# Neighbourhood attention in blocks of 8x8 queries of two heads, inside a kernel of attention and state-space layers

## The chip, the cores and the metric

The kernel runs on one core of one Trainium2 chip. The core has five engines that run side by side, each with its own queue in fixed order: TensorE (PE, matrix products; its weight loads are shown apart as PEld), VectorE (DVE), ScalarE (ACT), GpSimd (POOL) and SyncE (SP, which here only issues transfers). The metric is the device time of one launch in microseconds (us), as the median of several runs.

## The reference

```python
x = x + L0(_gn(x), w_qkv, w_out)      # x: (2, 48, 48, 768) float32
x = x + L1(_gn(x), in_proj_w, ...)    # group norm over 32 groups of 24 channels
...
# L0: 12 heads of 64; each query sees a 7x7 window of keys, clipped at the image's edge
scores = jnp.einsum('nhije,nhiajbe->nhijab', q, kg)
attn = jax.nn.softmax(scores.reshape(B, nh, H, W, K * K), axis=-1)
o = jnp.einsum('nhijab,nhiajbe->nhije', attn, vg)
return o @ w_out
...
# L1, for both directions of the 2304 tokens, 1536 channels, 16 states:
#   x, z = in_proj(x); x = silu(causal conv of 4 taps)
#   delta = softplus(dt_proj(x_proj(x)))
h = dA * h + (d_t * u_t)[..., None] * B_t[:, None, :]
y = jnp.einsum('bdn,bn->bd', h, C_t)
#   out = out_proj((y_forward + y_backward) * silu(z))
```

## The kernel before

**Order.** The kernel does not issue its work as it goes. Every piece of work is handed to a planner (class `Order`, line 94) with its engine, a cost in ns, a key (its due place, counted in units of the scan), and the buffers that it reads and writes. `Order.run` (line 153) then simulates the engines on these costs, and of the works that are ready takes the one that can start first, with the lower key ahead; works marked `job` fill in beside the main ones, but none more than 2.5 units ahead of the main work (`horizon`, line 170). The result is one fixed order of instructions on each engine. Where the planner sees PE without work for over 0.8 us in the scan, it puts idle transposes there (line 1491). On the chip, semaphores alone decide when an instruction starts; a fetch into a fresh buffer waits for nothing but its place in SP's queue.

**Stages.** Image 0's group norm and attention come first, with nothing beside them. Then DVE and POOL run the scan of image 0, forward and backward (1152 scan instructions of two states each on DVE, line 1258), and beside much of it, as jobs, the whole attention of image 1 (keys 50 to 118 units, `A1`) and then image 1's input projection and convolution (`in_proj`, from unit 118). Then the scan of image 1 follows, 1152 more. A scan unit is one channel tile of 128 in one chunk of 384 tokens: four groups of four states. In each group DVE or POOL fills `hb` (line 1225; the planner may choose the engine), ACT makes the decays in PSUM (line 1247), DVE scans, POOL multiplies by C (line 1273), and PE adds up by transposes into `py` (line 1290).

**Attention** (line 529). For every band of eight image rows (`t`, six bands, 384 queries) `project` makes queries, keys and values by matmuls (`product`, line 382) and spills them to HBM. `core(t)` goes over three groups `g` of two head pairs; it loads 14 rows of keys for the group (line 671) and its queries, and calls `block` for three blocks `u` of 8x16 queries. A block sees 14x22 = 308 keys, in three chunks of five, five and four rows (110, 110 and 88 keys). `block` fetches the values of the chunks (line 740) and a mask of 128 x 308 (line 751), and calls `heads` for each of the two head pairs. `heads` works on the two heads of a pair apart, each with 128 queries on the partitions:

- scores (line 769): one matmul for each head, 64 rows of the array, 128 queries by 308 keys, each head into a PSUM bank of its own
- DVE adds the mask and takes the minimum of the negated sum (line 779), ACT takes exponentials with their sum (line 785), DVE inverts the sum (line 800), DVE (image 0, line 816) or ACT (image 1, line 810) scales
- PE transposes three chunks a head into a bank (line 825); ACT copies the first two, and DVE (image 0) or ACT (image 1) the third (line 832)
- values (line 856): three chunks by two heads, each matmul 64 channels by 128 queries; the copy of the result is line 866

So each pair and block is two masks, two exponentials, two scalings, four copies, six transposes. For image 0 scores have both banks of `das[0]`, and transposes both of `das[1]` (`two`, line 536); for image 1 all share the tag `mm` with two banks, and scores and transposes take two of them at a time. Values of image 1 lie in the `uz` buffers beside the keys.

After the core, line 382 with `mm_ao` is the output projection, line 705 adds the input, line 710 takes statistics for the next group norm.

**Group norm** (line 427). Statistics of all tiles are aggregated (line 443); PE sums the channels of a group by a first matrix `gs` (line 448), and spreads the group's mean and later its scale back over channels by a second one, `gT` (line 457), which SP fetches (line 431). The planner lets that fetch follow the aggregation.

Of the kernel before, what the change touches and what calls it, by code (L numbers as in the profile page):

```python
# [26 lines left out]
QR, QC = 8, 16  # L27
WR, WC = QR + KN - 1, QC + KN - 1
NKEY = WR * WC
KR = 5  # L30
KCH = tuple((r * WC, min(KR, WR - r) * WC) for r in range(0, WR, KR))
# [26 lines left out]
def neighbourhood_masks():  # L58


    out = np.full((3, 3, QR, QC, WR, WC), NEG, np.float32)
    for a, t in enumerate((0, 1, HW // QR - 1)):
        for u in range(HW // QC):
            kr, kc = window(t, QR, WR), window(u, QC, WC)
            for r in range(QR):
                sr = min(max(t * QR + r - KN // 2, 0), HW - KN) - kr
                for c in range(QC):
                    sc = min(max(u * QC + c - KN // 2, 0), HW - KN) - kc
                    out[a, u, r, c, sr : sr + KN, sc : sc + KN] = 0.0
    return out.reshape(9, P, NKEY)  # L70
# [175 lines left out]
def tile_kernel(  # L246
# [61 lines left out]
    def cols(l0, cl, k0=0, nk=1):  # L308
# [6 lines left out]
        "w": 5, "u": 2, "dtw": 2, "dlt": 2, "hb": 7, "uz": 2, "vt": 3, "ev": 4, "pr": 4, "pT": 2,  # L315
# [111 lines left out]
    def group_norm(stats, n, key, job):  # L427
# [62 lines left out]
        for i, (eng, ns, fn, r, w) in enumerate((  # L490
            ("DVE", 600, aggregate, [stats], [mv]),
            ("SP", 400, fetch, [mv], [gT]),
# [36 lines left out]
    def attention(b, start, end, job, T):  # L529
# [6 lines left out]
        def two(what, n):  # L536

            if T[what] == "mm":
                return [ps("mm", f"{what}{n}_{j}") for j in range(2)]
            return [(das[T[what]], j) for j in range(2)]  # L540
# [14 lines left out]
        def project(t):  # L555
# [18 lines left out]
            for p in range(NP):  # L574
                for s in range(2):
# [10 lines left out]
                    if s == 0:  # L586
# [4 lines left out]
                                e.ap.rearrange("p (u r c) -> p u r c", u=HW // QC, r=QR),  # L591
                                acc[:, :TB].rearrange("p (r u c) -> p u r c", u=HW // QC, r=QR),
# [47 lines left out]
        def core(t):  # L640
# [12 lines left out]
            for g in range(NP // PG):  # L653
# [5 lines left out]
                nv = len(KCH) * PG * P if kv else 0  # L659
                ks = sb(tag("k", g), [P, nk + nv], f"k{n}", parts=2)  # L660

                vs = [(ks, 1, nk)]
                if kv:
                    more = sb(tag("k", g), [P, (HW // QC - 1) * nv], f"kv{n}", parts=HW // QC - 1)
                    vs += [(more, u, u * nv) for u in range(HW // QC - 1)]
# [10 lines left out]
                def queries(qs=qs, rows=rows):  # L676
# [4 lines left out]
                    w=[(ks, 0), *(v[0] for v in vs[1:])], size=PG * P * WR * HW * 4, **S,  # L681
# [5 lines left out]
                for u in range(HW // QC):  # L687
                    block(t, g, u, kr, rc, near, ks, vs, qs, oT, kg + u * slot * 0.8 / NP * PG / 3)
# [32 lines left out]
        def block(t, g, u, kr, rc, near, ks, kvs, qs, oT, key):  # L721

            kc = window(u, QC, WC)
            n = f"{b}_{t}_{g}_{u}"
            if "v" in T:
                vs, v0 = (sb(tag("v", u), [P, len(KCH) * PG * P], f"v{n}"), 0), 0
            else:
                vs, v0 = kvs[u][:2], kvs[u][2]
            vat = lambda p0, p1, k, c0, c1: vs[0][
                p0:p1, v0 + k * PG * P + c0 : v0 + k * PG * P + c1  # L730
            ]
            mask = sb("mask", [P, NKEY], n)
# [3 lines left out]
            def values():  # L736
                grid = vd[b].ap.rearrange("(h w) e -> h w e", w=HW)
                for k, (c0, nk) in enumerate(KCH):
                    r0 = kr + KR * k
                    nc.sync.dma_start(  # L740
                        vat(0, nk, k, 0, PG * P),
                        grid[r0 : r0 + nk // WC, kc : kc + WC, cs],
                    )

            add(
                "SP", 400 * len(KCH), values, key - 0.5,
                r=[(vd[b], [h * NTB + x for h in halves for x in near])], w=[vs],
                size=NKEY * PG * P * 4, **S,
            )
            add(  # L750
                "SP", 400, lambda: nc.sync.dma_start(mask.ap, masks[rc * 3 + u]), key - 0.5, w=[mask],
                size=P * NKEY * 4, **S,
            )
            for i in range(PG):
                p = g * PG + i
                heads(f"{n}_{i}", p, i, u, kc, ks, qs, vs, vat, mask, oT[p], key + 0.001 * i)

        def heads(n, p, i, u, kc, ks, qs, vs, vat, mask, to, key):

            sc, pts = two("s", n), two("pt", n)  # L760
            pr = [sb("pr", [P, NKEY], f"{n}_{j}") for j in range(2)]
            pT = sb("pT", [P, len(KCH), 2, P], n, parts=2)
            sm = sb("sm", [P, 4], n, parts=4)
            grid = lambda h: ks[h, i * WR * HW : (i + 1) * WR * HW].rearrange("p (r w) -> p r w", w=HW)[:, :, kc : kc + WC]

            def scores():
                for j in range(2):
                    h = slice(j * E, (j + 1) * E)
                    nc.tensor.matmul(
                        bank(sc[j], NKEY), qs[h, i, u * P : (u + 1) * P], grid(h), start=True,  # L770
                        stop=True,
                    )

            add("PE", mm(1, NKEY) * 1.2, scores, key, r=[(ks, 0), qs], w=[*sc, *pr], **S)
            for j in range(2):

                def masked(j=j):

                    nc.vector.tensor_tensor_reduce(  # L779
                        pr[j].ap, bank(sc[j], NKEY), mask.ap, -1.0, 3.0e38, ALU.add, ALU.min,  # L780
                        sm[:, j : j + 1],
                    )

                def exponentials(j=j):
                    nc.scalar.activation(  # L785
                        pr[j].ap, pr[j].ap, AF.Exp, bias=sm[:, j : j + 1], scale=-1.0,
                        accum_out=sm[:, 2 + j : 3 + j],
                    )

                add("DVE", dve(NKEY), masked, key, r=[sc[j], mask], w=[pr[j], (sm, j)], **S)  # L790
                add(
                    "ACT", act(NKEY, 1) + 90, exponentials, key, r=[pr[j], (sm, j)],
                    w=[pr[j], (sm, 2 + j)], **S,
                )

                if j or not job:
                    of = range(2 if job else 2 + j, 3 + j)
# [7 lines left out]
            for j in range(2):  # L805
                if job:

                    add(
                        "ACT", act(NKEY, 1),
                        lambda j=j: nc.scalar.mul(pr[j].ap, pr[j].ap, sm[:, 2 + j : 3 + j]), key,  # L810
                        r=[pr[j], (sm, 2 + j)], w=[pr[j]], **S,
                    )
                else:
                    add(
                        "DVE", 300,
                        lambda j=j: nc.vector.tensor_scalar_mul(
                            pr[j].ap, pr[j].ap, sm[:, 2 + j : 3 + j]
                        ),
                        key, r=[pr[j], (sm, 2 + j)], w=[pr[j]], **S,
                    )  # L820
                pt = pts[j]

                def turned(j=j, pt=pt):
                    for k, (c0, nk) in enumerate(KCH):
                        nc.tensor.transpose(  # L825
                            bank(pt, 512 - P)[:nk, k * P : (k + 1) * P], pr[j][:, c0 : c0 + nk],
                            ident,
                        )

                def taken(ks, copy, j=j, pt=pt):  # L830
                    nk = KCH[ks.start][1]
                    copy(
                        pT[:nk, ks, j, :],
                        bank(pt, 512 - P)[:nk, ks.start * P : ks.stop * P].rearrange(
                            "p (k q) -> p k q", q=P
                        ),
                    )

# [703 lines left out]
```

## Time and profile before

| | us |
|---|---|
| median of 3 runs (lowest, highest) | 7038.78 (7036.31, 7051.21) |
| the profiled execution: its span, from first to last instruction | 7054.5 |
| DVE, PE, POOL, ACT busy in the span | 6061.2, 6334.5, 5447.5, 4970.2 |
| scan, line 1258: 2304 x 1.746 us | 3924.9 |
| POOL's multiplication, line 1273: 1152 x 3.186 us | 3653.7 |
| fills, line 1225: POOL 495 x 3.203 us, DVE 657 x 1.743 us | 1584.6, 1141.4 |
| idle transposes, line 1491: 4431 | 550.4 |

The profiled execution is 15.7 us longer than the median of the runs. Its own time is known by its span only. In the profile a group is a line, an engine and an operation, with the names of output and inputs; a bracket behind an instruction gives the idle time of its engine before it and what ended that time. PE's ends are modelled, so that neighbours overlap a little: cadences are taken from start to start. A window row gives, for each engine, the busy time in the stretch and the number of instructions.

### The profile page before, as it was taken

The numbers are of one execution on the slowest core, as the hardware profiler recorded it, in microseconds if no ns is written. First come the engines' busy times: TensorE is split into PE (matmuls) and PEld (weight loads), VectorE is DVE, ScalarE is ACT, GpSimd is POOL, SyncE is SP. The second block draws the span as 40 slices with busy tenths as digits, with TensorE's granted clock in tenths as the row PEclk, the third lists the DMA queues.
The fourth block names the chain that finished last, engine by engine and source line by source line (L and its number), as shares of the span: only waits on it lengthen the run. The fifth ranks groups of instructions, "written<-read, shape, count | busy, mean of one in ns | idle before, by whom it ended". The sixth has DMA issues, their size and how long they took to land.

```text
span 7054.5 us, 105645 instructions
## 1 busy us (share of the span) xinstructions
PE 6334.5 (90%) x38151; PEld 4844.6 (69%) x38151; DVE 6061.2 (86%) x6217; ACT 4970.2 (70%) x10948; POOL 5447.5 (77%) x1951
## 2 busy tenths in 40 slices
PE   7999989999989998999988888888888898999888
PEld 5666656666667776676666656666678887777777
DVE  2354449999999999998898999999999999999998
ACT  1333248788887788887888778788876667777765
POOL 0000008888989999988898878999999999999997
PEclk9999989999999999999999999999999999999999
DMA  6565454444556444555444354343466676655553
GB/s 190 172 200 172 139 161 131 134 144 151 157 160 191 151 149 141 152 170 150 126 144 131 113 166 127 107 143 108 140 179 191 174 220 199 191 177 158 162 169 105
DMA packets 1337698, 1101.32 MB, mean 156 GB/s; under 512 B 136328, under 2 KB 1327416, under 8 KB 1337144
## 3 DMA queue, kind: packets, MB, share of 16 engines
q1 hardware_dynamic: 1337176, 1094.56, 52.1%
q8 instruction: 303, 4.96, 0.3%
q14 instruction: 219, 1.79, 0.1%
HBM read 881.41 MB, written 213.57 MB: 155 GB/s over the span
## 4 chain that ended last, share of the span: by engine, by line
DVE 39%; PE 19%; ACT 14%; POOL 12%; issue 9%; DMA 6%; SPq 1%; DVEq 0%; POOLq 0%; ACTq 0%
DVE hb L1258 25%; POOL hb L1273 8%; DVE hb L1225 7%; ACT da L1247 4%; PE mm_qk L382 4%; DVE uz_u L935 4%; POOL hb L1225 3%; PE py L1290 2%; PE mm_ao L382 2%; PE mm_v L382 2%; PE mm_xin L382 2%; ACT uz_u L928 1%; PE da L825 1%; ACT pr L785 1%; ACT L1163 1%
## 5 line engine op out<-in xcount | busy, mean ns | idle before, releaser
L1258 DVE TENSOR_TENSOR_SCAN hb<-da,hb 128x772 f32<-128x772 f32 x2304 | 3924.9, 1746 | 187.3 <-ACT da L1247 155.1
L1273 POOL TENSOR_TENSOR hb<-hb,bc 128x1536 f32<-128x1536 f32 x1152 | 3653.7, 3186 | 381.0 <-DVE hb L1258 338.3
L1247 ACT ACTIVATE da<-dlt,A 128x384 f32<-128x384 f32 x4608 | 2677.2, 584 | 915.2 <-DVE hb L1258 845.8
L1290 PE MATMUL py<-ident,hb 128*128 128x128 f32 x13824 | 1754.3, 279 | 264.3 <-POOL hb L1273 255.2
L1290 PEld LDWEIGHTS py<-ident,hb 128*128 128x128 f32 x13824 | 1570.9, 143 | 523.5 <-POOL hb L1273 413.6
L1225 POOL TENSOR_TENSOR hb<-u,bc 128x1544 f32<-128x1544 f32 x495 | 1584.6, 3203 | 22.6 <-PE py L1290 14.9
L1225 DVE TENSOR_TENSOR hb<-du,bc 128x1544 f32<-128x1544 f32 x657 | 1141.4, 1743 | 34.3 <-ACT du L1202 24.8
L1175 POOL TENSOR_TENSOR u<-dlt,u 128x384 f32<-128x384 f32 x288 | 263.8, 918 | 532.7 <-DMA bc<-xdf 412.6
L382 PE MATMUL mm_xin<-xc,w_x 128*128 128x390 f32 x1656 | 593.3, 504 | 25.3 <-DVE uz_u L935 16.2
L382 PE MATMUL mm_z<-xc,w_z 128*128 128x384 f32 x1728 | 608.1, 492 | 7.8 <-ACT dlt L1157 4.9
L382 PE MATMUL mm_out<-stage_y,w_o 128*128 128x192 f32 x3168 | 560.7, 332 | 18.1 <-ACT dlt L1157 6.4
L1491 PE MATMUL py<-ident 128*128 128x128 f32 x4431 | 550.4, 277 | 0.0
L382 PEld LDWEIGHTS mm_out<-stage_y,w_o 128*128 128x128 f32 x3168 | 522.0, 194 | 29.3 <-ACT dlt L1157 10.6
L1491 PEld LDWEIGHTS py<-ident 128*128 128x128 f32 x4431 | 503.3, 143 | 28.9 <-issue 26.0
L901 POOL MEMSET xc<- 128x18 f32 x4 | 0.5, 116 | 637.2 <-DVE sm L779 637.2
L382 PEld LDWEIGHTS mm_xin<-xc,w_x 128*128 128x128 f32 x1656 | 311.3, 195 | 238.3 <-issue 36.7
L935 DVE SCALAR_TENSOR_TENSOR uz_u<-mm_xin,conv_w,uz_u 128x384 f32<-128x384 f32 x792 | 428.3, 607 | 52.0 <-ACT uz_u L928 49.4
L382 PE MATMUL mm_qk<-xc_xn,w_qk 128*128 128x384 f32 x1296 | 459.1, 500 | 14.7 <-DMA w_qk<-in_w_qkv 3.1
L382 PEld LDWEIGHTS mm_z<-xc,w_z 128*128 128x128 f32 x1728 | 314.3, 192 | 194.4 <-issue 8.9
L382 PEld LDWEIGHTS mm_qk<-xc_xn,w_qk 128*128 128x128 f32 x1296 | 240.2, 194 | 173.8 <-issue 19.5
L785 ACT ACTIVATE pr<-pr,sm 128x308 f32<-128x308 f32 x432 | 234.5, 544 | 127.5 <-DVE sm L779 127.2
L1306 PE MATMUL py<-ident,vt 128*128 128x128 f32 x864 | 156.3, 292 | 146.3 <-ACT yt L1316 145.9
(163 smaller groups left out, 6780.9 us busy)
## 6 DMA issues: line engine op xcount, KB each, us to landing
w_o<-in_w_opT SPq DMA_DIRECT2D x264, 384.0 KB
bc<-xdf SPq DMA_DIRECT2D x96, 768.0 KB
bc<-xdb SPq DMA_DIRECT2D x96, 768.0 KB
w_qk<-in_w_qkv SPq DMA_DIRECT2D x144, 384.0 KB
w_x<-in_w_inT SPq DMA_DIRECT2D x144, 384.0 KB
w_z<-in_w_inT SPq DMA_DIRECT2D x144, 384.0 KB
w_ao<-in_w_out SPq DMA_DIRECT2D x72, 384.0 KB
u<-uf SPq DMA_DIRECT2D x48, 576.0 KB
```

The lines of the kernel that those rows point to most:

```text
L382: nc.tensor.matmul(acc[:m, o0 : o0 + cl], wb[:, wi, wo : wo + m], xb[:, xi, xo : xo + cl], start=c == 0, stop=c == n - 1,)
L785: nc.scalar.activation(pr[j].ap, pr[j].ap, AF.Exp, bias=sm[:, j : j + 1], scale=-1.0, accum_out=sm[:, 2 + j : 3 + j],)
L825: nc.tensor.transpose(bank(pt, 512 - P)[:nk, k * P : (k + 1) * P], pr[j][:, c0 : c0 + nk], ident,)
L935: nc.vector.scalar_tensor_tensor(u, px[:, at[j] : at[j] + cl], q["conv_w"][:, k, j : j + 1], u, ALU.mult, ALU.add,)
L1175: lambda j=j: nc.gpsimd.tensor_mul(u[:, j, h], dl[:, j, c], u[:, j, h]), at + 0.06 + 0.25 * j,
L1225: on.tensor_mul(cells(hb, SG), by.unsqueeze(1).to_broadcast([P, SG, W]), bc[g].ap)
L1247: lambda: nc.scalar.activation(cells(da, 2)[:, j % 2, h], dl[:, jd, c], AF.Exp, scale=q["A"][:, k, i : i + 1]),
L1258: lambda: nc.vector.tensor_tensor_scan(flip(hb[at2]), flip(da[:, : 2 * W]), flip(hb[at2]), 0.0, ALU.mult, ALU.add),
L1273: lambda: nc.gpsimd.tensor_mul(cells(hb, SG)[:, :, h], cells(hb, SG)[:, :, h], bc[NSG + g][:, :, c]),
L1290: nc.tensor.matmul(py[:tp, t * P : (t + 1) * P], cells(hb, SG)[:, j, h][:, tb[t]], ident, start=False, stop=g == NSG - 1 and j == SG - 1 a ...
L1306: nc.tensor.matmul(py[:tp, t * P : (t + 1) * P], vt[:, tb[t]], ident, start=t == 0, stop=False, is_transpose=True, skip_group_check=True,)
L1491: nc.tensor.matmul(marks["py"][:, CL : CL + P], ident, ident, start=False, stop=False, is_transpose=True, skip_group_check=True,)
```

## The change

Blocks become 8x8 queries with 14x14 = 196 keys in two chunks of seven rows (98 keys). The 64 queries of both heads of a pair stand together on the 128 partitions. `heads` handles two neighbouring blocks (`UU = 2`) at a time, so that it still covers 8x16 queries of a head pair, and `block` is called as often as before.

- Scores are four matmuls of 64 queries by 196 keys. The two heads use different rows and columns of the array, and write to different halves of the partitions of one bank, in which both blocks lie.
- Masks, exponentials and scalings stay two for each call, each 128 x 196 in place of 128 x 308; two inverses are as before.
- Four transposes take the place of six. Their copies are one of 512 columns on ACT (image 1), or one of 256 on ACT and one of 256 on DVE (image 0), in place of four.
- The value matmuls are eight, 64 channels by 64 queries, in place of six, 64 by 128.
- Scores and transposes take one bank each (`one`): of `das` in turn, or one of the tag `mm`.
- Value fetches are four of 98 keys in place of three; the mask is 128 x 392. For image 1 three of the twelve value pieces lie beside the keys and nine in the second buffer.
- `pr` has three buffers, each for both blocks, in place of four for one head each. The planner's costs for these works are changed with them.
- In the group norms of image 0, the fetch of `gT` follows a given tile's statistics (`near`) and not the aggregation.

```diff
-QR, QC = 8, 16
+QR, QC = 8, 8
+NQ = QR * QC
+NU = HW // QC
...
-KR = 5
-KCH = tuple((r * WC, min(KR, WR - r) * WC) for r in range(0, WR, KR))
+KR = 7
+KCH = tuple((r * WC, KR * WC) for r in range(0, WR, KR))
+NK = len(KCH)
+UU = 2
...
-    def group_norm(stats, n, key, job):
+    def group_norm(stats, n, key, job, near=None):
...
-            ("SP", 400, fetch, [mv], [gT]),
+            ("SP", 400, fetch, [mv] if near is None else [(stats, near)], [gT]),
...
-        def two(what, n):
+        def one(what, n):
 
             if T[what] == "mm":
-                return [ps("mm", f"{what}{n}_{j}") for j in range(2)]
-            return [(das[T[what]], j) for j in range(2)]
+                return ps("mm", f"{what}{n}")
+            i = turns[what] = turns.get(what, -1) + 1
+            return das[T[what]], i % 2
...
             def scores():
-                for j in range(2):
-                    h = slice(j * E, (j + 1) * E)
-                    nc.tensor.matmul(
-                        bank(sc[j], NKEY), qs[h, i, u * P : (u + 1) * P], grid(h), start=True,
-                        stop=True,
-                    )
+                for v in range(UU):
+                    for j in range(2):
+                        h = slice(j * E, (j + 1) * E)
+                        at = (u * UU + v) * NQ
+                        nc.tensor.matmul(
+                            scv(v)[j * NQ : (j + 1) * NQ], qs[h, i, at : at + NQ], grid(h, kcs[v]),
+                            start=True, stop=True,
+                        )
...
                     nc.vector.tensor_tensor_reduce(
-                        pr[j].ap, bank(sc[j], NKEY), mask.ap, -1.0, 3.0e38, ALU.add, ALU.min,
-                        sm[:, j : j + 1],
-                    )
+                        pr[:, v, :], scv(v), mask[:, v * NKEY : (v + 1) * NKEY], -1.0, 3.0e38,
+                        ALU.add, ALU.min, sm[:, v : v + 1],
+                    )
...
+            if job:
+                add("PE", UU * NK * 110 + 60, lambda: turned(range(UU)), key, r=[pr], w=[pt, pT], **S)
+                add(
+                    "ACT", act(UU * NK * P) + 30, lambda: taken(range(UU), nc.scalar.copy), key, r=[pt],
+                    w=[pT], **S,
+                )
+            else:
+                for v in range(UU):
+                    add(
+                        "PE", NK * 120 + 60, lambda v=v: turned([v]), key,
+                        r=[(pr, v), *([pt] if v else [])], w=[pt, (pT, v)], **S,
+                    )
+                for v, (eng, copy) in enumerate((("ACT", nc.scalar.copy), ("DVE", nc.vector.tensor_copy))):
+                    add(
+                        eng, act(NK * P) + 60, lambda v=v, copy=copy: taken(range(v, v + 1), copy), key,
+                        r=[pt], w=[(pT, v)], **S,
+                    )
...
-                for k, (c0, nk) in enumerate(KCH):
-                    for j in range(2):
-                        e0 = i * P + j * E
-                        nc.tensor.matmul(
-                            po[j * E : (j + 1) * E, :P], vat(0, nk, k, e0, e0 + E), pT[:nk, k, j, :],
-                            start=k == 0, stop=k == len(KCH) - 1,
-                        )
...
+                for v in range(UU):
                     for k, (c0, nk) in enumerate(KCH):
+                        for j in range(2):
+                            e0 = i * P + j * E
+                            nc.tensor.matmul(
+                                po[j * E : (j + 1) * E, v * NQ : (v + 1) * NQ],
+                                vat(v, k, nk, e0, e0 + E), pT[:nk, v, k, j * NQ : (j + 1) * NQ],
+                                start=k == 0, stop=k == NK - 1,
+                            )
...
-        norms.append(group_norm(stats2, f"b{b}", end, job))
+        norms.append(group_norm(stats2, f"b{b}", end, job, None if b else (NC - 2) * NTB - 1))
...
-        norms0.append(group_norm(s0, f"a{b}", A0[0] - 1 + 22 * b, b > 0))
+        norms0.append(group_norm(s0, f"a{b}", A0[0] - 1 + 22 * b, b > 0, None if b else NTB - 2))
```

## The prediction

> **What bounds the kernel now.** I read the chain of work that ended last first, then busy time by stretch, then single engines. The chain over the whole span:
>
> ```profile
> DVE 39%; PE 19%; ACT 14%; POOL 12%; issue 9%; DMA 6%; SPq 1%; DVEq 0%; POOLq 0%; ACTq 0%
> ```
>
> PE's share lies mostly in the first 950 us, image 0's attention, where nothing else can run yet. There PE works without a gap in the order of its instructions (start, length, line, count):
>
> ```profile
> 521.31 0.88 PE L856 MATMUL py_po<-pT,bc_v 110*64 110x128 f32 x12
> 522.12 0.87 PE L825 MATMUL da<-ident,pr 128*110 128x128 f32 x6
> 522.91 0.79 PE L769 MATMUL da<-hb_k,bc_q 64*128 64x308 f32 x4
> 523.63 2.20 PE L382 MATMUL mm_qk<-xc_xn,w_qk 128*128 128x384 f32 x6
> ...
> 28.35 0.54 SPq L431 DMA_DIRECT2D w_gTa<-c_gmatT  x1
> ...
> 34.93 2.69 PE L457 MATMUL mm_gna<-gn_ga,w_gTa 32*128 32x1 f32 x12 [5.60 <-DMA w_gTa<-c_gmatT]
> ...
> 951.41 2.68 PE L457 MATMUL mm_gnb<-gn_gb,w_gTb 32*128 32x1 f32 x12 [5.16 <-DMA w_gTb<-c_gmatT]
> ```
>
> From start to start, one pair of heads on one block costs PE 0.81 us (values), 0.79 (transposes) and 0.72 (scores), 2.32 in all; every fp32 matmul is two records, a transpose one. Between 44.6 and 943.7 PE is busy 861.2 of 899.1 us. The last two lines are the group norms' wait for the second matrix, with no other work to cover it.
>
> After that DVE bounds, with POOL close behind (they share the fills, L1225). I cut the time of image 1's attention at scan counts (L1258), since the scans are the same before and after: 576, 864, 1152 and 1248 scans end at 2582, 3344, 4172 and 4464 us. Busy time by engine there, and in a stretch without attention:
>
> ```profile
> core 0: us, PE busy (x) PEld busy (x) DVE busy (x) ACT busy (x) POOL busy (x), PEclk, DMA share, GB/s
> 2582.00:3344.00 762.00, 697.13 (x4431) 517.42 (x4429) 698.52 (x661) 609.99 (x1518) 674.43 (x240) 0.98 0.50 152
> 3344.00:4172.00 828.00, 733.83 (x4896) 545.45 (x4897) 762.73 (x866) 684.65 (x1745) 701.02 (x248) 0.98 0.45 136
> 4172.00:4464.00 292.00, 249.03 (x1381) 187.37 (x1380) 270.93 (x259) 223.50 (x398) 246.22 (x90) 0.92 0.44 136
> ...
> 5000.00:6750.00 1750.00, 1562.66 (x10034) 1346.18 (x10033) 1688.25 (x1180) 1299.19 (x2748) 1673.10 (x600) 0.97 0.62 179
> ```
>
> DVE is idle 8.3%, 7.9% and 7.2% there against 3.5% in the undisturbed stretch. In the chain between 4020 and 4330 us, image 1's input projection is now and then the last thing to end:
>
> ```profile
> 4053.44 7.87 PE mm_xin L382 x24
> ...
> 4202.55 9.59 PE mm_xin L382 x24
> ```
>
> It is late because attention is: in the order of DVE's instructions before, the last mask of image 1 stands at scan 1078 and its last statistics at 1095 of the 1152 that belong to image 0, so the convolutions (L935) crowd in at scans 1104 to 1200.
>
> **What the Trainium skill says.** "TensorEngine Tiling (Array Packing)", Restrictions and Gotchas: different row tiles cannot access one PSUM bank at the same time. This is the point of danger: the two heads' scores are now row tiles of one bank. "PSUM — Partial Sum Buffer", the section on bank collisions, is narrower: each bank of each partition is a RAM of its own, other quadrants of a bank may be used at once, and the hardware neither arbitrates nor stalls. The two heads write partitions 0–63 and 64–127. The trace before shows row tiles overlapping in two banks (L769) and column tiles overlapping in one (L856), not the mix. "TensorE: Matmul & The Clock Gate", LDWEIGHTS: a load costs columns / 1.2 ns, whatever the rows. The trace agrees: twelve 64-column loads of L856 take 0.64 us, 53 ns each.
>
> **The change on PE.** A record of 384 columns takes 0.355 us in a half product (2.13/6), 0.92 ns a column.
> - Scores: before, two passes of both heads side by side, 0.36 us each: 308 columns (0.28) plus about 0.08 that is a 128-column load not hidden. After: four passes of 196 columns (0.18) with a 64-column load (0.04), 0.88 us: +0.16. If the load is hidden 0.72, +0.0; if the tiles don't overlap, 8 x 0.21 = 1.67, +0.95.
> - Transposes: four for six at 0.132 us: −0.26.
> - Values: 16 records for 12, each 64 columns wide instead of 128. Before 67 ns each, of which 53 is the load. After, the load sets the pace: 16 x 60 = 0.96, +0.15. Bounds: 16 x 40 = 0.64 (loads of two column tiles overlap), −0.17, and 16 x 67 = 1.07, +0.26.
> - Sum +0.05 a block, 2.37; bounds −0.4 and +0.2 with overlap.
>
> **First stage.** 108 blocks: +5 us on PE. The 37.9 us of PE idleness: scores waiting for the masks of the block before (5.9), transposes for its copies (6.8) and for reciprocals (3.9) go in part, since scores and transposed weights take one bank in turn and not both: −6. In the stretches without projections (794–840, 863–918) blocks follow at 2.93 us because DVE needs 3.04 a block: masks 2 x 0.55, reciprocals 2 x 0.16, scaling 2 x 0.38, copies 2 x 0.28 and 0.29. At 1.06 ns an element (copies of 128 and 384 columns, 283 and 554 ns) it needs 2.43: masks and scaling −0.12 each, and one 256-column copy of 0.42 for two. PE is then the longer; about 18 blocks x 0.45 = −8. The values' DMA of each third block is waited for there (10.8 us in all); four issues at 0.72 us for three put it 0.7 later, under +4. Group norm: the planner's new precondition moves the fetch within SP's queue, where it itself waits for nothing. For a0 it stands behind the fetch of the first matrix (19.50 us) and ahead of the first tile's fetch (27.93, which waits for a statistics buffer), so at about 20.1 instead of 28.35; with 6.4 us to landing it is there before 29.5, when the spread could start: −5.4, and the first tile's fetch behind it loses nothing. For b0 it stands behind the store of the fourth updated tile (936.5) instead of behind the fetch of the first convolution tile (944.65): −5.0. Sum: +5 −6 −8 +4 −10 = −15; bounds −70 (PE's block at its low bound) and +15.
>
> **Second stage.** DVE: 216 masks, 112 elements shorter, 0.117 us each: −25. In the built order 7 fills go from DVE to POOL: −12 on DVE, +22 on POOL, which has room. ACT loses some 110 us (exponentials and scaling 432 x 0.09, one 512-column copy of about 0.6 for four copies of 1.27 together). The last statistics now stand at scan 956 instead of 1095, and the work moves accordingly (blocks, convolution taps counted in the order):
> - Scans 529 to 576 (118 us): 12 blocks for 7, +3.
> - To 864: 65 blocks for 41. PE 695 + 24 x 2.37 = 752; DVE 698 + 65 x 0.74 − 41 x 0.97 − 6 fills x 1.74 = 696. PE becomes the limit; at the 96% it reached in the first stage, 783: +21. Bounds: 762 (0) and 93%, 809 (+47).
> - To 1152: 31 blocks for 60, 156 taps for 102. DVE 763 − 35 + 54 x 0.54 − 3 = 754; PE falls to some 610 without its idle transposes (94 us of L1491). At 5% idle 794: −34. Bounds: 3% −51, 8% −8.
> - To 1248: 78 taps for 132. DVE 271 − 29 + 3 = 245; at 5% idle 258: −34. Bounds −39 and −25.
> - Behind it the order is the same. The values' and masks' bytes grow by 14 MB of 1101, and 108 issues on SP: hidden, the DMA share is 0.45 to 0.50.
>
> Sum −44, bounds −87 and +17. With the first stage −59: the profiled execution would have a span of 6995. It lies 0.22% above the median of the runs; the median becomes 7038.8 x 6995.5/7054.5 = 6980.
>
> **Rivals.**
> - R1, slower: the scores' quadrants do not overlap since they share a bank. +0.79 us a block over my estimate: 108 blocks in the first stage, +85, and the 77 blocks up to scan 864, where PE is the limit, +61. −59 + 146 = +87: 7126. It decides from +0.32 us a block on (59/185). For it: the first page named; against it: the second, and L856.
> - R2, PE's load eats the gain: compressing the attention costs +47 up to scan 864, and the later stretches keep their 8% idleness (−33); values cost 1.07 us (+12 in the first stage). +17 −3: +14, 7053. For it: PE has no idle transposes in that stretch before (2 us); against it: late blocks there waited for one another, not for PE.
> - R3, more: DVE goes to 3% idle, PE holds 98.7%, values are at the low bound (−34 in the first stage). −87 −49: 6903. For it: "mm" buffers, three a block for five, on which the deltas and the sums of both directions also wait (DVE waits 22 us for L1343 during attention).
> - R4, only the norms' waits count, −10: 7029, within 0.2%. Against it: 23 us of DVE idleness at scans 1152 to 1248 alone.
>
> **How the numbers follow.** Main case 0.58 (6930 to 7015), R1 0.09, R2 0.11, R3 0.18, R4 0.04. Differences under 0.2% (14 us) cannot be told from none. The range 6905 to 7050 leaves out R1, the upper half of R2 and the tail of R3. Faster: main and R3, with a little of R2, 0.77; same: R4 and half of R2, 0.10; slower: R1 and the rest, 0.13.
>
> **What would show it.** Scores (four passes a block) near 0.88 us start to start: R1 is dead; 1.6: R1. Values near 0.96. PE's spread of gna and gnb without a DMA wait. The first input convolution about 925 to 945 us. The last statistics of image 1 near 3600 us at scan 956, PE above 95% before scan 864, DVE idle 5% from there to scan 1248 and no stall on the input projection. If PE is under 93% before scan 864 and that stretch is still longer, something that I don't see (a buffer or SP's queue) holds the blocks. Scans after 1248 should take the same time as before.

## The result, and the profile after

The changed kernel takes 7049.87 us (median of 6 runs, 7039.69 to 7067.49), the kernel before 7037.55 us (6 runs, 7034.64 to 7051.21): a ratio of 1.0009, 95% interval 0.9992 to 1.0026. A repetition with more runs (12 of the changed kernel, 39 of the one before) gave 0.9995, 0.9986 to 1.0003. The change makes no difference that can be measured; 6980 us were predicted. The kernel before was timed anew with every set of runs, and its median moved between sets from 7037.55 to 7056.75 us, so across sets only ratios compare.

The two profiled executions have spans of 7054.5 us before and 7038.2 us after. The first lies above its kernel's median and the second below, so their difference of −16 us says nothing of the verdict. Where the time lies, stretch by stretch, does repeat: in the second profile of the changed kernel every stretch is within 3 us of the first. The stretch ahead of scan 1 is the exception. With one and the same order of instructions on DVE it took 1057 and 1049 us in two profiles with the old blocks, and 1014 to 1031 in eight with the new ones, where the mean granted clock ahead of scan 1 was 0.966 at 1014 us and 0.955 at 1031. So the −36 of the table stands for something between −18 and −42. The scans are the same in both kernels, and cut the span at the same points of the work (us):

| scans | before | after | difference | predicted |
|---|---|---|---|---|
| ahead of scan 1 | 1057 | 1021 | −36 | −15 |
| 1 to 529 | 1406 | 1404 | −2 | 0 |
| 529 to 576 | 116 | 128 | +12 | +3 |
| 576 to 864 | 764 | 849 | **+85** | **+21** |
| 864 to 1152 | 829 | 794 | −35 | −34 |
| 1152 to 1248 | 292 | 251 | −41 | −34 |
| 1248 to 2304 | 2552 | 2553 | +1 | 0 |

Five of the seven rows are as predicted or better. The row to scan 576 is 9 us worse than predicted, and the one to scan 864 is 64 us worse and takes the whole gain back.

The order of PE in image 0's attention (start, length, line, count, and in brackets PE's idle time and what ended it), the counterpart of the lines of before:

```profile
521.33 1.54 PE L784 MATMUL da<-hb_k,bc_q 64*64 64x196 f32 x16
522.80 2.20 PE L387 MATMUL mm_qk<-xc_xn,w_qk 128*128 128x384 f32 x6
524.84 0.60 PE L825 MATMUL da<-ident,pr 128*98 128x128 f32 x4
...
527.93 0.69 PE L879 MATMUL py_po<-pT,bc_v 98*64 98x64 f32 x16
528.55 0.42 PE L825 MATMUL da<-ident,pr 128*98 128x128 f32 x2
528.90 0.88 PE L784 MATMUL da<-hb_k,bc_q 64*64 64x196 f32 x8
529.71 0.69 PE L879 MATMUL du_po<-pT,bc_v 98*64 98x64 f32 x16
```

As in the prediction, a block here is one call of `heads`: one pair of heads on 8x16 queries. The first line is the scores of two such blocks, and the next instruction begins 1.47 us later: 0.735 us for one. A single one takes 0.81 from start to start (528.90 to 529.71). The values' sixteen records take 0.62 us (527.93 to 528.55), 39 ns each. Four transposes at the 0.13 us of before would be about 0.52. Together a block costs PE some 1.95 us, against 2.32 before.

The group norms (SP's queue and PE, the same columns):

```profile
20.23 0.53 SPq L436 DMA_DIRECT2D w_gTa<-c_gmatT  x1
...
29.71 2.72 PE L462 MATMUL mm_gna<-gn_ga,w_gTa 32*128 32x1 f32 x12 [0.24 <-DVE gn_ga L484]
...
914.57 2.71 PE L462 MATMUL mm_gnb<-gn_gb,w_gTb 32*128 32x1 f32 x12 [0.24 <-DVE gn_gb L484]
```

Both waits for the second matrix are gone: before, PE stood 5.60 and 5.16 us there.

Busy time in the stretches (length, then busy us and number of instructions of each engine); the first three end at scans 864, 1152 and 1248, the last is the stretch without attention:

```profile
core 0: us, PE busy (x) PEld busy (x) DVE busy (x) ACT busy (x) POOL busy (x), PEclk, DMA share, GB/s
2554.00:3402.00 848.00, 777.55 (x5496) 583.55 (x5495) 714.21 (x802) 632.96 (x1578) 685.48 (x243) 0.97 0.53 162
3402.00:4196.00 794.00, 676.65 (x4944) 535.57 (x4943) 747.17 (x751) 614.62 (x1373) 715.63 (x256) 0.97 0.44 134
4196.00:4448.00 252.00, 214.86 (x1441) 172.13 (x1440) 245.59 (x206) 191.38 (x358) 238.66 (x85) 0.99 0.36 110
5000.00:6750.00 1750.00, 1561.83 (x10052) 1349.21 (x10053) 1691.98 (x1180) 1295.59 (x2744) 1674.03 (x600) 0.97 0.61 178
```

In the first row no engine is full: PE is busy 91.7%, DVE 84.2%, POOL 80.8%. Before, the same 288 scans had 91.5%, 91.7% and 88.5%. Of PE's 677 us in the second row 145 are idle transposes (94 of 734 before): right behind the stretch where PE is short of room, it has room left. In the third row DVE is idle 2.5% (7.2% before): the stall ahead of the input projection is gone.

The chain of work that ended last is of no help here, and its shares say so:

```profile
DVE 18%; POOL 5%; issue 5%; ACT 4%; PE 3%; DMA 1%; DVEq 0%; SPq 0%; POOLq 0%; ACTq 0%
```

They add up to 36%, the last 2540 us: followed back, the chain of this profile breaks off at 4498 us. What is late between scans 576 and 864 has to be read from the waits of single engines there (total, times, longest, in us). Before:

```profile
DVE hb L1258 <- ACT da L1247: 24.4, 20, 5.0
DVE pr L779 <- PE mm_s L769: 15.4, 8, 5.8
DVE sm L800 <- ACT pr L785: 0.2, 1, 0.2
...
POOL hb L1273 <- DVE hb L1258: 55.9, 34, 7.2
POOL hb L1225 <- PE py L1290: 11.3, 5, 4.6
```

After:

```profile
DVE hb L1287 <- ACT da L1276: 30.2, 28, 3.3
DVE pr L794 <- PE mm_s L784: 21.3, 13, 9.0
DVE xr_x L712 <- PE mm_ao L387: 15.2, 8, 3.3
DVE sm L815 <- ACT pr L800: 15.0, 21, 3.0
...
DVE pr L794 <- DMA mask<-c_masks: 5.3, 2, 4.7
...
POOL hb L1302 <- DVE hb L1287: 67.8, 40, 6.0
POOL hb L1254 <- PE py L1319: 42.6, 11, 8.3
```

DVE waits more for PE and ACT at the steps of attention, POOL more for PE's sums: many waits of about one to four microseconds in the mean, the longest of these lines 9.0, no single large one. Transfers have a small part (5.3 us for masks).

### The profile page after: what moved, and what is told of

The parts are those of the page before. It is cut to its first block, busy times and chain, and to the rows that moved or that the text cites. A ratio compares the mean times of both kernels' runs of the same rounds, so it can differ in the third digit from the quotient of the medians.

```text
span 7038.2 us, 108877 instructions
## 1 busy us (share of the span) xinstructions
PE 6280.1 (89%) x40140; PEld 4878.2 (69%) x40140; DVE 5990.5 (85%) x6102; ACT 4851.3 (69%) x10516; POOL 5468.5 (78%) x1958
## 5 line engine op out<-in xcount | busy, mean ns | idle before, releaser
L1254 POOL TENSOR_TENSOR hb<-u,bc 128x1544 f32<-128x1544 f32 x502 | 1606.8, 3203 | 48.7 <-PE py L1319 42.6
L1520 PE MATMUL py<-ident 128*128 128x128 f32 x5124 | 630.8, 277 | 0.0
L1520 PEld LDWEIGHTS py<-ident 128*128 128x128 f32 x5124 | 586.8, 143 | 17.3 <-issue 13.6
L1260 ACT COPY bc<-state 128x8 f32<-128x8 f32 x960 | 183.0, 196 | 143.9 <-DVE hb L1254 68.3
L800 ACT ACTIVATE pr<-pr,sm 128x196 f32<-128x196 f32 x432 | 194.0, 450 | 126.4 <-DVE sm L794 124.8
```

Of the source, the lines that this page charges most:

```text
L800: nc.scalar.activation(pr[:, v, :], pr[:, v, :], AF.Exp, bias=sm[:, v : v + 1], scale=-1.0, accum_out=sm[:, UU + v : UU + v + 1],)
L1254: on.tensor_mul(cells(hb, SG), by.unsqueeze(1).to_broadcast([P, SG, W]), bc[g].ap)
L1260: "ACT", 98, lambda: nc.scalar.copy(bc[g][:, :, ends], was), now - 0.4,
L1520: nc.tensor.matmul(marks["py"][:, CL : CL + P], ident, ident, start=False, stop=False, is_transpose=True, skip_group_check=True,)
```

## The experiments

**Which image loses.** Two kernels use the new blocks for one image only; both have the new place of the group norms' fetch. The image with the old blocks needs other buffers for `pr` (and in the first run the new masks lie in `xpw`).

```diff
# img0: image 1 keeps the blocks of 8x16
-            attention(b, *A1, True, BESIDE)
+            attention_old(b, *A1, True, BESIDE)
# img1: image 0 keeps them
-    attention(0, *A0, False, FIRST)
+    attention_old(0, *A0, False, FIRST)
```

> The change in image 0's attention and in the group norms alone; image 1's attention is that of the kernel before, in its old order. Theory A (the first stage gains some 35 us, and image 1's attention, moved forward in the scan, costs it again): about 7003 us (6990 to 7012), scan 1 at about 1020 us and every later stretch as before. Rival B (the gain of the first stage does not last: the scan's stretches lengthen whatever image 1 does): 7030 to 7045.

> The change in image 1's attention and in the group norms alone; image 0's attention is that of the kernel before. Theory A: slower, 7060 to 7085, since scans 529 to 864 take some 95 us more and scans 864 to 1248 some 75 us less. Rival B (image 1's part is harmless): 7025 to 7045.

Measured: new blocks for image 0 alone, 7025.81 against 7056.75 us, ratio 0.9957 (0.9940 to 0.9973). For image 1 alone, 7073.68, ratio 1.0025 (1.0016 to 1.0034). The times that were expected count from 7037.55 us; the kernel before took 19 us more in this set, so differences are compared. Image 0 gains 31 us (A expected about 35, B at most 8), and it is not given back later. Image 1 loses 17, although its run has the norms' new fetch too; A had expected a loss of 22 to 47, B at most 7. In the first the stretches are 116, 766, 824 and 289 us between scans 529, 576, 864, 1152 and 1248, within 5 us those of the kernel before; in the second they are 124, 849, 797 and 251, those of the changed kernel. The whole loss is image 1's attention beside the scan.

**A slower pace, first try.** If 65 blocks are too many between scans 576 and 864, later due times should help. In two runs the due times of attention (`A1`) and of the input projection behind it (`P1`) were moved together.

```diff
-    A0, A1, P1 = (-56, -16), (50, 118), 118
# pace_50_130
+    A0, A1, P1 = (-56, -16), (50, 130), 130
# pace_42_128
+    A0, A1, P1 = (-56, -16), (42, 128), 128
```

> The changed kernel with image 1's attention due over units 50 to 130 and its input projection from 130, instead of 50 to 118. The last statistics stand at scan 1041 instead of 956 (1095 in the kernel before). Theory A (PE's work was moved to where PE is the limit): scans 576 to 864 take about 800 us instead of 848, and the whole 7015 to 7035. Rival C (the new blocks are slower beside the scan in themselves, by a buffer or by the values' transfers, whatever their pace): 7045 to 7060, the loss only moves.

> The changed kernel with image 1's attention due over units 42 to 128, the widest of all: first masks at scan 498, last statistics at 1023. Theory A: PE's load is the most even, 6995 to 7025. Rival C: 7045 to 7060.

Both theories missed by far: ratios 1.0270 (1.0254 to 1.0285) and 1.0227 (1.0211 to 1.0242). The stretch in question did what it should, 775 and 752 us in place of 849. But scans 1536 to 2304, in which attention has no part, took 2094 and 2070 us in place of 1814: `P1` also sets when each later chunk of image 1 goes through the input projection, and image 1's scan waited for it. In the first of the two runs 120 records of the input projection (`mm_xin`) stand between scans 1536 and 2304, where the changed kernel has none, and POOL waits there once for 268.7 us for the deltas of a tile. The runs changed two things at once, and the second hid the first.

**A slower pace alone.** The next two leave `P1` where it was.

```diff
-    A0, A1, P1 = (-56, -16), (50, 118), 118
# end_128
+    A0, A1, P1 = (-56, -16), (50, 128), 118
# wide_42_128
+    A0, A1, P1 = (-56, -16), (42, 128), 118
```

> The changed kernel with image 1's attention due over units 50 to 128, and the input projection from unit 118 as it was. 54 blocks and 18 output projection tiles between scans 576 and 864 instead of 65 and 24. Theory A (PE is the limit there, at 91.5% busy): some 47 us of PE less, so that stretch about 798 us; 864 to 1152 some 805; the whole about 40 us less than the changed kernel. Rival C (the new blocks are slower beside the scan in themselves): within 15 us of the changed kernel.

> The changed kernel with image 1's attention due over units 42 to 128, the input projection from unit 118 as it was. Theory A: 25 to 60 us less than the changed kernel; scans 1 to 576 lose some 20 us, for five blocks and a band's projections stand there, and scans 576 to 864 take 770 to 795. Rival C: within 15 us of the changed kernel.

Measured: `end_128` 0.9967 (0.9957 to 0.9978), 7032.51 us, and `wide_42_128` 0.9882 (0.9867 to 0.9897), 6968.48 us; the kernel before took 7054.9 and the changed kernel 7052.78 in this set. Both gain more on the changed kernel than the 15 us of rival C. Theory A has the sign right and the sizes wrong: 20 us for about 40, since scans 864 to 1152 took 853 us for 805, and 84 for 25 to 60. The second run is 1.2% faster than the kernel before, with the new blocks unchanged. Stretches from scan 1 to 1248 (us), and blocks by the order of DVE's instructions:

| scans | before | after | end_128 | wide_42_128 |
|---|---|---|---|---|
| 1 to 529 | 1406 | 1404 | 1412 | 1426 |
| 529 to 576 | 116 | 128 | 126 | 122 |
| 576 to 864 (blocks) | 764 (41) | 849 (65) | 767 (54) | 748 (54) |
| 864 to 1152 (blocks) | 829 (60) | 794 (31) | 853 (42) | 801 (36) |
| 1152 to 1248 | 292 | 251 | 246 | 244 |
| sum | 3407 | 3426 | 3404 | 3341 |

The crowded stretch loses 82 to 101 us. Eleven blocks fewer, at about 2 us of PE each, do not explain that by themselves. Busy time there, `end_128` first, then `wide_42_128`:

```profile
2570.00:3337.00 767.00, 691.07 (x5011) 524.35 (x5009) 692.21 (x725) 602.52 (x1493) 683.68 (x241) 0.96 0.53 161
```

```profile
2577.00:3325.00 748.00, 688.73 (x5002) 523.20 (x5001) 692.45 (x731) 604.34 (x1496) 698.66 (x248) 0.98 0.55 166
```

PE's busy time falls from 777.55 us by 86 and 89, about as much as the stretch itself: with the blocks, projections of the neighbouring bands leave it too (180 of 828 records of `mm_v`, some 100 of 543 of `mm_qk`, 72 and 48 of 288 of `mm_ao`). In `end_128` much of this work lands between scans 864 and 1152, which take 59 us more. In `wide_42_128` PE, DVE and POOL are all at 92 to 93% in the crowded stretch, where the changed kernel has 92, 84 and 81.

**Is it PE's work?** Read as a sum, PE looks like the limit of the crowded stretch. The next kernel keeps the order of the changed one, instruction by instruction, and takes three of the six products out of each of image 1's output projections. By count that is 77 us of PE, 51 of them between scans 576 and 864; in the trace the busy time of `mm_ao` in this stretch falls by 42 us, from 98.5 to 56.2.

```diff
-                for c in range(c0, c0 + 3):
+                for c in range(c0, c0 if half and c0 else c0 + 3):
...
-                        start=c == 0, stop=c == n - 1,
+                        start=c == 0, stop=c == (2 if half else n - 1),
```

> The changed kernel, its order kept, but each output projection of image 1's attention leaves out three of its six products (2.13 us of PE for each of 36 tiles, 77 us in all, 24 tiles of them between scans 576 and 864); nothing is left out on another engine. Theory A: scans 576 to 864 take about 55 us less (51 us at 91.5%), and 864 to 1152 stays within 15 us, since DVE is the limit there. Rival C: both stretches stay within 15 us.

> The changed kernel itself, on the same chip as the next three. From the first six pairs of runs: 0.995 to 1.002 of the kernel before. Stretches as in its first profile: scans 576 to 864 about 849 us, 864 to 1152 about 794, 1152 to 1248 about 251.

Measured: less_pe 0.9986 (0.9979 to 0.9992), 7043.78 us; the changed kernel again, 0.9995 (0.9986 to 1.0003), 7052.78 us. Of 77 us, 6 (by the ratios) to 9 (by the medians) come back. The stretch takes 845 us (850 in the repetition), so theory A's 55 us did not come, and rival C's numbers did, though C itself fell with the two runs above:

```profile
2556.00:3401.00 845.00, 743.68 (x5355) 561.63 (x5354) 715.31 (x803) 631.75 (x1578) 687.02 (x244) 0.96 0.54 163
```

PE is busy 34 us less than in the changed kernel and idle 31 us more. The granted clock was 0.96 here and 0.97 there; on 744 us that is worth some 8 us (an estimate from these figures), too little to hide a gain of 55. What was freed turned into idle time of PE. So the stretch is not PE's throughput in an order that is already fixed, and the plain form of that explanation falls.

**Is it the order, then?** The order is made ahead of time from the planner's costs. Two runs let the planner make it anew for less PE work. One tells it what less_pe leaves out. The other changes one number and nothing of the work: the change had given the values' product a cost of 900 ns, and the chip takes 0.62 us.

```diff
# val620
-                "PE", 900, weighted, key, ...
+                "PE", 620, weighted, key, ...
# less_pe_plan: less_pe, and
-                "PE", mm(3, cl), part, key, ...
+                "PE", 10 if half and c0 else mm(3, cl), part, key, ...
```

> Changes one number of the changed kernel: the planner's cost of the value product, 900 ns (times 1.05) to 620; the chip took 0.62 us. The work is the same, only the order is made anew. C, the order is made around a PE that the planner takes for fuller than it is, and an order once made cannot be shortened by freeing PE alone (which would explain that leaving out 77 us of PE in a kept order changed nothing): 65 blocks x 0.31 us = 20 us less in the stretch of scans 576 to 864, so 825 to 830 for 849, the later stretches within 10 us; ratio to before 0.995 to 0.998. D, the stretch is set by the hops of the blocks from engine to engine and the two banks of mm, however PE is priced: 845 to 853, ratio 0.998 to 1.001.

> As the run less_pe (each output projection of image 1 leaves out three of its six products, so the output differs from the reference), but the planner is told so and makes its order for the smaller work. C, PE's capacity is what the order was made around: with 51 us less PE work between scans 576 and 864 that stretch takes 790 to 805, against 845 with the order kept; the stretch to scan 1152 785 to 800; ratio to before 0.990 to 0.993. D, hops and banks set it: 835 to 850 as in less_pe, ratio 0.997 to 1.000.

> The changed kernel with the value product's cost at 620 ns and image 1's attention due from unit 46 to 128 in place of 50 to 118 (17 blocks before scan 576, 55 to 864, 36 to 1152). The run with 42 to 128 had stretches of 1426, 122, 748, 801 and 244 us. C: a start four units later gives back half of the 22 us that the first of these lost, and the truer cost some 5 to 15 us in the next ones: ratio to before 0.983 to 0.987. D: the truer cost does nothing and the start alone gives 0.986 to 0.990.

Measured: val620 0.9940 (0.9924 to 0.9956), 7004.97 us; less_pe_plan 0.9930 (0.9915 to 0.9945). The stretch up to scan 864, val620 first, then less_pe_plan:

```profile
2549.00:3370.00 821.00, 768.50 (x5574) 576.60 (x5573) 712.73 (x802) 635.57 (x1592) 695.60 (x247) 0.99 0.56 170
```

```profile
2550.00:3360.00 810.00, 737.09 (x5438) 558.98 (x5437) 712.71 (x802) 632.64 (x1587) 693.69 (x246) 0.97 0.56 171
```

Theory C held in both against D. In val620 the same work, 65 blocks in the same 288 scans, takes 821 us for 849, slightly more off than C expected. Not all of these 28 us need be the order's: PE is busy 9 us less for the same work, at a granted clock of 0.99 for 0.97. Scans 1152 to 1248 took 239 us for 251, which C had not expected. In less_pe_plan the same work as in less_pe takes 810 for 845, a little short of the 790 to 805 expected. So the time hangs on the order as well as on the work, and PE's room, as the planner reckons it, is part of what shapes the order. In the other 14 profiles, in which each order was made for its own work, PE is busy 89.5 to 93.6% of this stretch; only in less_pe, with work taken out of an order that stayed, does its share fall to 88.0%. PE's work therefore remains a fair measure of the stretch, as long as the order is made for it. A planner's cost changed at random, without regard to PE, was not run, so how much of a gain any other order could bring is not known.

The third run of this set, a pace of 46 to 128 with the truer cost, gave 0.9903 (0.9887 to 0.9920): neither C's 0.983 to 0.987 nor, at its median, D's 0.986 to 0.990, and no better than 42 to 128 without it. Its stretches are 1409, 127, 763, 822 and 252 us from scan 1 to 1248. So one more run took both the pace of `wide_42_128` and the truer cost:

```diff
-                "PE", 900, weighted, key, ...
+                "PE", 620, weighted, key, ...
...
-    A0, A1, P1 = (-56, -16), (50, 118), 118
+    A0, A1, P1 = (-56, -16), (42, 128), 118
```

> The changed kernel with the value product's cost at 620 ns and image 1's attention due from unit 42 to 128 (18 blocks before scan 576, 62 to 864, 28 to 1152), in one run what gave 0.9882 (42 to 128 alone) and 0.994 (620 alone). C, the truer cost gains wherever PE is nearly full: with 62 blocks up to scan 864 that stretch stays under 765 us and the next under 790, ratio 0.983 to 0.987. E, the truer cost helped only against an order that was too dense, and at an even pace nothing is left of it: 0.987 to 0.992, and the stretch to scan 864 is longer than the 748 us of 42 to 128 alone, since it holds 8 blocks more.

Measured: 0.9895 (0.9878 to 0.9911), as E expected in the ratio; the stretches are 1432, 124, 753, 812 and 253 us. The blocks were miscounted in that expectation: 54 stand up to scan 864 and 36 up to 1152, as in `wide_42_128`, so E's reason for a longer stretch does not apply. The truer cost helps where the order is too dense, and nothing of it is left at an even pace.

**Would the pace have helped the old blocks?**

```diff
# in the kernel before
-    A0, A1, P1 = (-56, -16), (50, 118), 118
+    A0, A1, P1 = (-56, -16), (42, 128), 118
```

> The kernel before with image 1's attention due from unit 42 to 128 in place of 50 to 118; its blocks stand at 9 before scan 576, 40 to 864, 59 to 1152 (before: 7, 41, 60), so the order has nearly the same pace: with the old blocks attention runs behind its due times whatever these are. F, the gain of the even pace needs the new blocks: ratio 0.997 to 1.003, the stretch 576 to 864 at 755 to 775. G, the due times themselves were wrong for both kernels: ratio 0.985 to 0.992.

Measured: 1.0030 (1.0018 to 1.0041), at the upper end of what F expected and far from G. Its stretch from 576 to 864 is 736 us, below F's range, but the one from 1152 to 1248 grows to 331, because the last statistics now stand at scan 1118 in place of 1095 and the input projection behind them comes late (DVE waits 36.6 us in this stretch for ACT's first step of the convolution, 9.8 before). A unit is eight scans, so the due ends of 118 and 128 units are scans 944 and 1024. The new blocks keep them (last statistics at scans 956 and 1023), and then the due times matter; the old ones lag behind both (1095 and 1118). Other due times for the old blocks were not run.

## Why the prediction was wrong

The mechanism was seen, and one term of the sum was mis-sized: **"To 864: 65 blocks for 41 ... at the 96% it reached in the first stage, 783: +21"**. It measured +85, outside even the bounds given (0 and +47). Three things were wrong in it.

- *PE's work.* The count took 24 blocks more at 2.37 us, +57. The output projections that move with the blocks were left out, although they stand in the same order. PE's busy time on `mm_ao`, before and after, in a view limited to that tile:

```profile
2579.00:3344.00 765.00, 48.41 (x144) 0.98 0.50 153
```

```profile
2554.00:3402.00 848.00, 98.53 (x288) 0.97 0.53 162
```

  That is +50, and the blocks themselves only +27 (the scores, transposes and values there went from 117 to 144 us). With the sum, +77 (the whole of PE's busy time went from 697 to 778), the stretch needs 810 us at 96%, which would be about +46.
- *The share that PE can reach.* 96% came from the first stage, which has no scan beside it; why it should hold beside the scan was not said. Beside the scan PE had 91.5% before, by the prediction's own table, and got 91.7%. At that share 777.6 us of work last 848. This is the other half of the miss, some 38 us.
- *Work divided by share holds only for an order made for that work.* less_pe took 34 us off PE's busy time and 3 us off the stretch, in the order that was there. With a new order for the same work the stretch took 810 us (less_pe_plan), and with the same work as the changed kernel in another order 821 (val620). That the engines wait for one another in their fixed queues is what the many small waits suggest; which waits a new order removes was not followed.

The other steps, in the prediction's order:

- *Scores 0.88 us, R1 dead if they overlap.* They overlap, at 0.735 to 0.81: R1's mechanism does not exist here. The page of the Trainium skill that R1 rested on ("TensorEngine Tiling (Array Packing)", Restrictions and Gotchas) says that row tiles cannot access one bank at the same time; in this kernel two row tiles that write different partitions of one bank do. "PSUM — Partial Sum Buffer", in its section on bank collisions, is less clear a witness than the prediction made of it: it allows other quadrants of a bank for two different engines, and for two writes of TensorE it repeats the first page's rule. But the collision of row tiles that it reports is one inside one bank and one quadrant (32 partitions), and this fits what was measured, for the two heads lie in different quadrants.
- *Values 0.96 us.* 0.62, the lower bound given. The price by "TensorE: Matmul & The Clock Gate", LDWEIGHTS, 53 ns for 64 columns, was used as if the loads of two column tiles came one after the other; a record and its load take 39 ns here, so they overlap. The prediction found the 53 ns in the trace before, but only as 0.64 us divided by twelve: in its single records the loads start in pairs, 6 to 8 ns apart, and the pairs follow every 109 ns, as the matmuls of 128 columns do. With 64 columns the pairs follow every 58 ns. So the matmuls set that pace and not the loads.
- *First stage −15.* −36 in this pair of profiles, −31 by the medians of img0. From the first projection to the second group norm (44.6 to 945.1 before, 39.4 to 913.2 after) 26.7 us came off. PE's busy time went from 861.2 to 820.4, and its idle time from 39.3 to 53.4 us. The prediction had idleness falling by 6; instead the transposes wait longer for DVE's copy of the bank before, 20.1 us for 6.8. The values' transfers cost 11.5 for 10.8, less than the +4 allowed.
- *Group norms −5.4 and −5.0.* The first projection begins 5.2 us earlier (44.61 to 39.42). From the second group norm's first product to the first input convolution it is 11.1 us for 16.0, −4.9. Right.
- *864 to 1152 −34, 1152 to 1248 −34.* −35 and −41. DVE's busy time in the two is 747 and 246 us (754 and 245 predicted), its idle share 5.9% and 2.5% where 5% was taken for both: right in the first, and 2 us past the bound of −39 in the second. PE's work without idle transposes is 531 us (677 less 145) where some 610 were expected: the output projections that were missing from the sum up to scan 864 are gone from this stretch, where `mm_ao` falls from 94 to 49 us.
- *"Behind it the order is the same."* +1 us over 1056 scans. Right.
- *R2* forecast 7053, beside the 7050 that came. It saw that compressed attention could cost more than it returns, but not by this sum: its +47 up to scan 864 is nearer than the +21 of the main case and still half of the 85, while the later stretches gained in full and values were cheaper, both against R2. That the totals meet is luck.
- *R3* had the values right (0.62, its low bound 0.64) and PE's share wrong: it needed 98.7%, and 93.6% is the most that any run here reached in that stretch.
- *"If PE is under 93% before scan 864 and that stretch is still longer, something that I don't see (a buffer or SP's queue) holds the blocks."* PE was at 91.7%, so the sign given was the right one. By the runs it is the order together with the work that it packs there. A third bank for `mm` was not tried, since all of PSUM is given away in this kernel. Of transfers the profile shows little: 5.3 us of DVE's waits (masks), 3.3 and 3.9 of PE's (keys, projection weights).

**What stays open.** Which of the many hops sets the crowded stretch was not separated; the runs show that the order decides together with the work that falls there, that PE's cost in the plan is one lever (28 us of that stretch, part of it perhaps the clock's) and the pace another (82 to 101 us of that stretch, 20 and 84 of the whole), and that the two do not add up.

## What to carry to other kernels

Where an order is fixed ahead of time, faster work arrives together with whatever hangs on it: count every instruction that moves into a stretch, and take the share that an engine can reach from the same kind of stretch. Freeing time on the busiest engine gave next to nothing here while the order stayed; after a change in costs, set the due times anew from the profile, so that no stretch is packed while the next one has room. Here new due times alone turned "no difference" into 1.2% (0.9882, at 42 to 128), and the old blocks did not gain from the same ones (1.0030). The planner's truer cost helped only at the dense pace (0.9940).

## What the runs showed of the hardware

- Matmuls on two 64 by 64 tiles of the array, with different rows and different columns, that write the two partition halves of one PSUM bank run side by side. In the single records of the trace the partners start 6 to 7 ns apart, and eight records of 196 columns take 0.735 us. A single pass of 196 columns is 0.18 (0.92 ns a column, from the projections), so eight in a row would be 1.44, an estimate.
- Matmuls on two column tiles, 64 columns each, follow every 39 ns with their loads (16 in 0.62 us), against 67 ns for 128 columns before: halving the width nearly halved the time of a record.
- The granted clock varied between runs of one program order: image 0's stage, with the same order of instructions on DVE, took 1014 us at a mean of 0.966 and 1031 us at 0.955.
